# A convolution network's third stage: one-pass spreads of split statistics, and a group mean taken from integers instead of from the activations

## The chip, the cores and the metric

The kernel runs on one core of one Trainium2 chip. The metric is the device time of one launch in microseconds, the median of three runs. The core's engines are named as in the profile: PE (TensorE) multiplies matrices, PEld is its weight load, DVE is VectorE, ACT is ScalarE, POOL is GpSimd, and SP only issues DMAs here. Each engine works off its own instructions in order and waits on semaphores for the others.

## The reference

x has the shape (8192, 8, 16, 16): samples, channels, height, width. Four residual layers follow one another; each normalizes in four groups of two channels (512 values) and convolves.

```python
x = x + L0(_gn(x))   # tensor-train product, bias
x = x + L1(_gn(x))   # 3x3 convolution, batch norm, relu
x = x + L2(_gn(x))   # q = clip(round(gn * 127/max|gn|)), integer 3x3 weights, / (sx * sw), bias
x = x + L3(_gn(x))   # 3x3 convolution, edge padding, weights sign(w) * mean|w|, bias
# _gn: (g - mean) / sqrt(var + 1e-5) over each group of a sample
```

Layer 2 needs the largest magnitude of the whole normalized tensor, and layer 1's batch norm needs all of its output, so the work falls into three stages with a global step between them.

## The kernel before, in words

A batch tile is 128 samples: 128 partitions (8 channels x 16 rows) by 2048 columns (128 samples x 16 columns of the image). There are NT = 64 tiles. A 3x3 convolution is three matrix products with a 128x128 band matrix, one for each horizontal shift, so that a tile takes four quarters of 512 columns (`BANK`) times three products.

*Stage one* runs layer 0 and the convolution of layer 1 on every tile. Constants that are needed later are made a few at a time between its steps by `late_constants`. *Stage two* applies batch norm and relu, adds, takes each group's statistics, centres x by the group mean (so that a group of x has mean zero from there on), keeps the statistics in `gnst`, and finds the largest normalized magnitude. Thirteen tiles stay in SBUF, the others go through DRAM. *Stage three* runs layers 2 and 3 on every tile and writes the output.

What stage three does to a tile, by the names in its table `OPS`:

- `rows2`, `spread2`, `v`, `q`: the group's scale 1/sigma is turned from a column into rows on DVE (`to_rows`: products with a mask into `diag`, then a 32x32-block transpose), spread by PE over the 128 partitions into PSUM (`r2`, tile `ps_a`), and DVE multiplies x by it into int8. ACT turns the int8 into bf16 `q`.
- `c2h0`, `c2h1`: six bf16 products each make one half of layer 2 in PSUM (`pq`). `bias` adds layer 2's bias to the first half of x on ACT and `stz` adds the product to it on DVE; the second half is scaled and biased out of PSUM by ACT (`z1`, into `z3`) and added on POOL (`add1`).
- `sq`, `sums`: ACT squares x, and PE sums x and its square over a group's partitions (`s`): for each of four quarters one fp32 product with 32 output columns, each quarter in a 32-column tile of its own of the array. `small` on DVE reduces over the image's columns and turns the result; `pow` on POOL makes 1/sigma.
- `rows3`, `spread3`: mean/sigma, 1/sigma and the stage-two mean go to rows in the same way (three `diag` products and a transpose) and are spread by two fp32 products into `r3` (`ps_r`) and `o3` (`ps_o`).
- `t`, `hi`, `edl`, `lo`: x times 1/sigma is split into two fp32r parts, the high part by ACT and the low part by POOL. `c` and `corr` add the constant part to x. `c3h0a` to `c3h1b` are 24 fp32r products with the sign matrix (`pf`), and `out0`, `out1` on DVE add them to x; SP writes the tile out.

The order of all this is written out by hand. `PHASE` gives each operation a time within a tile, `PERIOD` the distance of tiles, and the operations of all tiles are issued in order of `PERIOD * i + PHASE[op]`. Each engine keeps that order, since its calls go through the helper `InOrder` (line 43, the line that the profile shows for nearly everything). In PSUM, `pq` and `pf` share two buffers of two banks (`pc`), and `hi`, `lo`, `v`, `q` and `t` have two buffers each. Loads of tiles from DRAM are issued by SP four tiles ahead, at the operation that begins a tile.

Of the kernel before, what the change touches and what calls it, by code (L numbers as in the profile page):

```python
# [18 lines left out]
P = 128  # L19
# [13 lines left out]
class InOrder:  # L33
# [24 lines left out]
PACK2 = [("w2all", C * C * 9), ("w3all", C * C * 9)]  # L58


@with_exitstack
def tile_net(ctx: ExitStack, tc: tile.TileContext, xb, xt_in, pack0, pack1, pack2, out):
# [34 lines left out]

    LATE = 5 if NT >= KEEP + STAY + 3 else 0

    def load2(i, what="yx"):  # L100
# [46 lines left out]
    def late_constants(late):  # L147
# [103 lines left out]
        dve.memset(gpad, 0.0)  # L251
        dve.tensor_copy(gpad[:, :, 0:G], quarter.unsqueeze(1).to_broadcast([P, NQ, G]))
        for k, name in enumerate(("sel0", "sel1", "corr")):

            t = L[name] = const.tile([P, CH], F32, name=name)
            dve.tensor_copy(t.rearrange("p (g n) -> p g n", g=G),
                            mod32[:, G * k:G * k + G].unsqueeze(2).to_broadcast([P, G, CH // G]))
        yield "statistics"
# [442 lines left out]

    def stats_small(mv, st, ps, name):

        s = small.tile([P, 32], F32, name=f"s_{name}", tag="s")
        dve.tensor_reduce(s, samples(ps), AX.X, ALU.add)
        dve.transpose(st, s)
        sq = small.tile([P, G], F32, name=f"sq_{name}", tag="sqm")
        dve.tensor_copy(mv[:, 0:G], st[:, 0:G])
        dve.tensor_tensor(sq, st[:, 0:G], mv[:, 0:G], ALU.mult)
        dve.scalar_tensor_tensor(mv[:, G:2 * G], st[:, G:2 * G], EPS, sq, ALU.add, ALU.subtract)  # L710

    def stats_pow(mv):
# [19 lines left out]
    with tc.tile_pool(name="p2", bufs=2) as p2, tc.tile_pool(name="ps2", bufs=2, space=PSUM) as ps2:  # L732
# [31 lines left out]
        def stats2(i):  # L764

            st, mv = psc[:, 32 + 32 * (i % 2):64 + 32 * (i % 2)], gnst[:, order2[i]]
            red = small.tile([P, 32], F32, name=f"s_c{i}", tag="s")
            dve.tensor_reduce(red, samples(T[i].pop("ps")), AX.X, ALU.add)
            dve.transpose(st, red)
            T[i]["sq"] = small.tile([P, G], F32, name=f"sq_c{i}", tag="sqm")  # L770
            act.copy(mv[:, 0:G], st[:, 0:G])
            act.activation(T[i]["sq"], st[:, 0:G], AF.Square)

        def sigma2(i):
            st, mv = psc[:, 32 + 32 * (i % 2):64 + 32 * (i % 2)], gnst[:, order2[i]]
            dve.scalar_tensor_tensor(mv[:, G:2 * G], st[:, G:2 * G], EPS, T[i].pop("sq"), ALU.add, ALU.subtract)
            stats_pow(mv)

        def spread2(i):
            T[i]["gb"] = ps = ps2.tile([P, BANK], F32, name=f"gb_{i}", tag="gb")  # L780
            rows = to_rows(diag[i % 2], mask2, [gnst[:, order2[i]]], f"c{i}")
# [46 lines left out]
        for i in range(NT + 4):  # L828
# [4 lines left out]
            elif late:  # L833
                k, j = late.pop(0)
                T2[j][k] = y_used[i - 1]
                nc.sync.dma_start(T2[j][k], (x1_d if k == "x" else y_d)[order2[j]])
            on(i, sum2)
            on(i - 2, sums2)
# [11 lines left out]
    nc.vector.tensor_reduce(pm, amax, AX.X, ALU.max)  # L850
    nc.gpsimd.partition_all_reduce(gm, pm, P, bass_isa.ReduceOp.max)
    nc.vector.reciprocal(sx, gm)
    nc.vector.tensor_scalar(sx, sx, 127.0, None, ALU.mult)
    nc.vector.tensor_tensor(inv, sx, L["sw"], ALU.mult)
    nc.vector.reciprocal(inv, inv)

    gv = gnst[:, :, G:2 * G]
# [5 lines left out]
    with ExitStack() as s:  # L863
        wk = s.enter_context(tc.tile_pool(name="wk3", bufs=2))
        ps_c = s.enter_context(tc.tile_pool(name="ps_c3", bufs=2, space=PSUM))
        ps_s = s.enter_context(tc.tile_pool(name="ps_s3", bufs=1, space=PSUM))
        order = [*kept, *(t for t in range(NT) if t not in kept)]

        sq3, t3, z3 = sqs[0], [sqs[1], xh], [y_stay[3][:, h * F // 2:(h + 1) * F // 2] for h in range(2)]
        T = [dict() for _ in range(NT)]  # L870
        AHEAD = min(NT, KEEP - 6)
        diag2, diag3 = diagonal("d"), diagonal("e")
# [3 lines left out]
        put_quarter(ps_a[:, P:2 * P])  # L876
        mask, st3 = ps_a[:, P:P + NQ], ps_a[:, P + 32:P + 64]

# [55 lines left out]
        def first2(i):  # L934
            x = halves(T[i]["x"])[:, 0]
            dve.scalar_tensor_tensor(x, T[i].pop(("pq", 0)), inv, x, ALU.mult, ALU.add)

        def second2(i):
            act.activation(z3[i % 2], T[i].pop(("pq", 1)), AF.Identity, bias=L["bias2"], scale=inv)

        def add2(i):
            x = halves(T[i]["x"])[:, 1]
            pool.tensor_tensor(x, x, z3[i % 2], ALU.add)

# [3 lines left out]
        def sums3(i):  # L948
            T[i]["ps"] = ps_s.tile([P, BANK], F32, name=f"s3_{i}", tag="s3")
            sums_pe(T[i]["ps"], T[i]["x"], sq3)  # L950

        def stats3(i):
            T[i]["mv"] = small.tile([P, 2 * G], F32, name=f"mv3_{i}", tag="mv")
            stats_small(T[i]["mv"], st3, T[i].pop("ps"), f"d{i}")

        def pow3(i):
            stats_pow(T[i]["mv"])

# [43 lines left out]
        def finish(i, h):  # L1002
# [8 lines left out]
        OPS = {"rows2": rows2, "spread2": spread2, "v": scale2, "q": round2, "bias": bias2,  # L1011
               "c2h0": lambda i: layer2(i, 0), "stz": first2, "c2h1": lambda i: layer2(i, 1), "z1": second2, "add1": add2,
               "sq": square3, "sums": sums3, "small": stats3, "pow": pow3, "rows3": rows3, "spread3": spread3, "c": offset3,
               "t": scale3, "hi": high3, "lo": low3, "corr": add3, "edl": edges3,
               "c3h0a": lambda i: layer3(i, 0, 0), "c3h0b": lambda i: layer3(i, 0, 1), "out0": lambda i: finish(i, 0),
               "c3h1a": lambda i: layer3(i, 1, 0), "c3h1b": lambda i: layer3(i, 1, 1), "out1": lambda i: finish(i, 1)}
        todo = [(op, i) for _, op, i in sorted((PERIOD * i + at, op, i) for op, at in PHASE.items() for i in range(NT))]
# [75 lines left out]
```

## Time and profile before

| what | value |
|---|---|
| median of three runs | 3823.76 us (3823.36 to 3825.31) |
| the profiled execution: time, span | 3824.58 us, 3822.8 us |
| mean granted clock of PE | 0.962 |
| busy in the span: PE, DVE, ACT, POOL | 94%, 89%, 66%, 80% |
| stage two's last operation on DVE (`amax`) | starts at 3062.76 us |
| third stage's first `v` | starts at 3066.51 us |

The span runs from the first to the last instruction. The share of busy time over the whole span is an average of three stages with different limits, so the table is only a start: a change in one stage is read from that stage's own stretch of time, its own chain of waits and its own timeline.

### The profile page before, as it was taken

The numbers are of one execution on the slowest core, as the hardware profiler recorded it, in microseconds if no ns is written. First come the engines' busy times: TensorE is split into PE (matmuls) and PEld (weight loads), VectorE is DVE, ScalarE is ACT, GpSimd is POOL, SyncE is SP. The second block draws the span as 40 slices with busy tenths as digits, with TensorE's granted clock in tenths as the row PEclk, the third lists the DMA queues.
The fourth block names the chain that finished last, engine by engine and source line by source line (L and its number), as shares of the span: only waits on it lengthen the run. The fifth ranks groups of instructions, "written<-read, shape, count | busy, mean of one in ns | idle before, by whom it ended". The sixth has DMA issues, their size and how long they took to land.

```text
span 3822.8 us, 52777 instructions
## 1 busy us (share of the span) xinstructions
PE 3598.8 (94%) x16264; PEld 2127.1 (56%) x16326; DVE 3386.0 (89%) x6313; ACT 2518.2 (66%) x2676; POOL 3048.8 (80%) x3104
## 2 busy tenths in 40 slices
PE   8999999999999999999999999997665589999999
PEld 4666666666666666666666666663221145555555
DVE  8988888888888888888888888877998889999997
ACT  5666666666666666666666666665665578778775
POOL 4877777778777777787777777865887779999998
PEclk9999999999999999999999999998776689999999
DMA  5787787878877878878788878766999724444442
GB/s 212 254 270 256 258 269 252 265 258 258 271 253 261 272 253 262 262 250 272 254 263 270 257 258 265 253 200 253 419 424 424 326 90 186 182 183 187 181 161 110
DMA packets 210809, 960.93 MB, mean 251 GB/s; under 512 B 44896, under 2 KB 45152, under 8 KB 110048
## 3 DMA queue, kind: packets, MB, share of 16 engines
q1 hardware_dynamic: 173808, 692.22, 48.8%
q0 software_dynamic: 36288, 264.26, 23.5%
q8 instruction: 131, 2.15, 0.2%
q14 instruction: 150, 1.23, 0.1%
q10 hardware_dynamic: 432, 1.08, 0.1%
HBM read 578.84 MB, written 378.54 MB: 250 GB/s over the span
## 4 chain that ended last, share of the span: by engine, by line
PE 85%; DVE 6%; DMA 4%; issue 2%; POOL 1%; ACT 1%; POOLq 0%; SPq 0%; DVEq 0%; ACTq 0%
PE po L43 45%; PE pu L43 12%; PE pf L43 10%; PE pm L43 6%; PE pq L43 4%; PE s L43 3%; PE pc L43 3%; DVE top L43 3%; PE ps_r L43 1%; DMA ys<-x_d 1%; DMA x_d<-u 1%; DMA x_d<-ys 1%; DMA u<-x_d 1%; DMA x_d<-xs 1%; DMA sq<-y_d 1%
## 5 line engine op out<-in xcount | busy, mean ns | idle before, releaser
L43 PE MATMUL po<-u,core 128*128 128x512 f32 (+1 forms) x4112 | 1844.7, 591 | 0.0
L43 ACT COPY u<-pu 128x2048 f32<-128x2048 f32 x512 | 955.4, 1866 | 512.9 <-PE pu L43 512.8
L43 PEld LDWEIGHTS po<-u,core 128*128 128x128 f32 x4112 | 744.6, 190 | 737.0 <-issue 736.1
L43 PE MATMUL pu<-core2r,xl 128*128 128x256 f32 x4032 | 678.6, 310 | 4.5 <-ACT u L43 3.5
L43 PEld LDWEIGHTS pu<-core2r,xl 128*128 128x128 f32 x4032 | 527.9, 189 | 127.9 <-issue 123.1
L43 POOL TENSOR_TENSOR bs<-bs,xh 128x512 fp32r<-128x512 f32 (+1 forms) x253 | 325.1, 1285 | 203.0 <-ACT xh L43 203.0
L43 POOL TENSOR_TENSOR v<-e 128x128 f32<-128x128 f32 x750 | 396.7, 540 | 0.0
L43 DVE TENSOR_TENSOR xs<-po,xs 128x512 f32<-128x512 f32 x256 | 176.9, 691 | 218.8 <-PE po L43 218.6
L43 ACT ACTIVATE m<-pm,b 128x128 f32<-128x128 f32 x250 | 91.7, 367 | 395.3 <-PE pm L43 395.3
L43 PEld LDWEIGHTS pm<-v,fast 128*128 128x128 f32 x2000 | 262.5, 192 | 119.7 <-issue 105.7
L43 POOL TENSOR_TENSOR e<-x1n,x 128x512 f32<-128x512 f32 x250 | 305.9, 1223 | 23.2 <-ACT x L43 15.8
L43 DVE TENSOR_TENSOR bs<-bs,stat 128x1024 f32<-128x1024 f32 x252 | 290.6, 1215 | 2.1
L43 POOL TENSOR_TENSOR xs<-xs,w 128x2048 f32<-128x2048 f32 x64 | 291.4, 4552 | 0.6 <-DMA xs<-in_xt 0.6
L43 PE MATMUL pm<-v,fast 128*128 128x128 f32 x2000 | 263.6, 275 | 0.0
L43 ACT ACTIVATE x<-x1n 128x512 f32<-128x512 f32 x500 | 247.0, 545 | 7.6 <-DVE x1n L43 7.6
L43 POOL TENSOR_TENSOR mv<-mv,mhalf 128x4 f32<-128x4 f32 x127 | 130.8, 1030 | 135.9 <-DVE mv L43 135.9
L43 PE MATMUL pf<-hi,sign 128*128 128x512 f32 x768 | 231.1, 439 | 0.0
L43 POOL DMA_DIRECT2D xl<-limb_d x252 | 149.8, 594 | 101.3 <-ACT x L43 38.4
L43 PE MATMUL pf<-lo,sign 128*128 128x512 f32 x768 | 218.0, 422 | 0.3 <-ACT lo L43 0.3
L43 POOL TENSOR_TENSOR v<-r 128x128 f32<-128x128 f32 x500 | 215.2, 447 | 0.0
L43 ACT ACTIVATE sq<-xs 128x2048 f32<-128x2048 f32 x103 | 197.0, 1913 | 18.2 <-DVE xs L43 13.6
L43 PE MATMUL gb<-rows_c,sel 128*128 128x128 f32 x128 | 40.8, 413 | 166.3 <-DVE rows_c L43 166.3
(308 smaller groups left out, 7195.3 us busy)
## 6 DMA issues: line engine op xcount, KB each, us to landing
xl<-limb_d POOLq DMA_DIRECT2D x252, 1024.0 KB, 7.4
x_d<-xs SPq DMA_DIRECT2D x76, 1024.0 KB, 8.4
xs<-in_xt SPq DMA_DIRECT2D x64, 1024.0 KB, 7.6
bs<-in_xb SPq DMA_DIRECT2D x63, 1024.0 KB, 5.6
limb_d<-xh SPq DMA_DIRECT2D x1008, 64.0 KB, 4.4
limb_d<-bs SPq DMA_DIRECT2D x1008, 64.0 KB, 5.2
y_d<-ys SPq DMA_DIRECT2D x60, 1024.0 KB, 8.0
u<-x_d SPq DMA_DIRECT2D x34, 1024.0 KB, 6.5
```

What stands on the lines that cost most here:

```text
L43: return self.tc.keep_in_program_order(op(*args, **kwargs))
```

## The change

**Statistics to rows.** Mean/sigma, 1/sigma, the stage-two mean of tile i and the scale of tile i + 4 (`LEAD`) are gathered as 16 columns (`columns3`, ACT; `shift3`, DVE). They are split into a high half that fp32r holds exactly (`high_column3`, ACT) and the rest (`low_column3`, DVE), 32 columns in all. One fp32r product with the identity turns them into 32 rows in PSUM (`turn3`), ACT copies these out (`rows3`), and four fp32r products with 32 rows spread them (`spread3`). The mask, the `diag` products and the transposes of both old spreads go.

**The mean of layer 3's input.** Since a group of x has mean zero before layer 2, the sum over a group comes from layer 2's integers: products of bf16 `q` with band matrices whose output columns are summed by group (`total`, made by `group_weights` in stage two), less what the image's two edge columns have too much. That is eight bf16 products of 512 columns and sixteen of 32 columns in place of the four fp32 products with x. The squares are summed as before. The group mean of the bias moves from layer 2's bias to layer 3's.

**Work moved between engines.** `SHARE` = 24 samples (384 columns) of layer 2's second half go the way of the first half: ACT's `bias` covers 1408 columns, DVE adds them (`third2`, named `stz1`), and `z1` and `add1` shrink to 640. The squared mean moves from DVE to ACT (`sqm`).

**Order.** `PHASE` and `PERIOD` are new, the second half of layer 2 and of layer 3 now comes ahead of the first, and the seven shared operations also run for tiles -4 to -1.

```diff
-PERIOD = 11.539
-PHASE = {"rows2": 0, "spread2": 0.01, "v": 5.1, "q": 10.2, "bias": 10.4, "c2h1": 11.6, "z1": 13.1, "c2h0": 16.1, "add1": 17.1,
-         "stz": 23.1, "sq": 24, "sums": 31.8, "small": 34.7, "pow": 37.3, "rows3": 42.7, "spread3": 45.3, "t": 46.3,
-         "hi": 49.9, "c": 51.2, "lo": 51.9, "corr": 58.8, "edl": 60.3, "c3h0a": 60.4, "c3h0b": 61.3, "out0": 66.8,
-         "c3h1a": 69.3, "c3h1b": 69.4, "out1": 69.41}
+PERIOD = 10.91
+PHASE = {"v": 0, "q": 5.5, "c2h1": 7.9, "bias": 10.7, "cols": 12.1, "stz1": 12.3, "c2h0": 13, "z1": 13.2, "stz": 14.4,
+         "add1": 16.1, "sq": 19, "sums": 20.4, "small": 24.9, "sqm": 26.2, "var": 26.21, "pow": 27.1, "mr": 29.5, "lhh": 31.8,
+         "lhl": 32.7, "turn": 33.6, "rows": 33.9, "spread": 36, "t": 37.2, "c": 43.8, "hi": 48.4, "lo": 49.3, "corr": 49.4,
+         "edl": 57.1, "c3h1a": 58.1, "c3h1b": 58.6, "c3h0a": 61, "c3h0b": 61.2, "out1": 62, "out0": 65.5}
+LEAD = 4
+SHARE = 24
...
+        pair = w["bias2all"].rearrange("p (g k) -> p g k", k=C // G)
+        dve.tensor_tensor(pair, pair, grp.unsqueeze(2).to_broadcast([P, G, C // G]), ALU.mult)
+        mb = const.tile([P, 1], F32, name="mb")
+        dve.tensor_reduce(mb, w["bias2all"], AX.X, ALU.add)
+        dve.tensor_scalar(mb, mb, 512.0 * G / C, None, ALU.mult)
+        dve.tensor_tensor(L["bias2"], L["bias2"], mb, ALU.subtract)
+        dve.tensor_tensor(L["bias3"], L["bias3"], mb, ALU.add)
...
+        def group_weights():
+            part = const.tile([P, 3, G], F32, name="part")
+            total = L["total"] = const.tile([P, 6, 32], BF16, name="total")
+            pool.memset(total, 0.0)
+            dve.tensor_reduce(part.rearrange("p k g -> p (k g)"), L["band2"].rearrange("p k (g n) -> p (k g) n", g=G), AX.X, ALU.add)
+            for k in range(0, 3, 2):
+                dve.tensor_tensor(part[:, 1], part[:, 1], part[:, k], ALU.add)
+                dve.tensor_scalar(part[:, k], part[:, k], -1.0, None, ALU.mult)
+            dve.tensor_copy(total[:, 0:3, 0:G], part)
+            dve.tensor_tensor(total[:, 3:6, 0:G], part, total[:, 0:3, 0:G], ALU.subtract)
...
     nc.gpsimd.partition_all_reduce(gm, pm, P, bass_isa.ReduceOp.max)
...
+    K3 = 8 * G
+    identr = wk.tile([P, P], F32R, name="identr", bufs=1)
+    back2, back3, high, low = (wk.tile([K3, CH], F32R, name=n, bufs=1) for n in ("back2", "back3", "corr_h", "corr_l"))
+    L["select"](back2, 3, 7)
+    L["select"](back3, 1, 5)
+    act.copy(high, L["corr"][0:K3])
+    act.copy(identr, ident)
+    dve.tensor_tensor(low, L["corr"][0:K3], high.bitcast(F32), ALU.subtract)
...
-        def rows2(i):
-            T[i]["rows2"] = to_rows(diag2[i % 2], mask, [gnst[:, order[i], G:2 * G]], f"d{i}")
+        def columns3(i):
+            T3[i] = col = wk.tile([P, 4 * G], F32, name=f"col_{i}", tag="col", bufs=4)
+            if i < 0:
+                for k in range(2):
+                    act.copy(col[:, 2 * G * k:2 * G * k + 2 * G], gnst[:, i + LEAD])
+            elif i + LEAD < NT:
+                act.copy(col[:, 2 * G:3 * G], gnst[:, i, 0:G])
+                act.copy(col[:, 3 * G:], gnst[:, i + LEAD, G:2 * G])
...
+        def shift3(i):
+            if i >= 0:
+                dve.scalar_tensor_tensor(column(i, 0), st3[:, 0:G], inv512, column(i, 1), ALU.mult, ALU.mult)
+
+        def high_column3(i):
+            act.copy(lhs[i % 2][:, 0:4 * G], T3[i])
+
+        def low_column3(i):
+            lh = lhs[i % 2]
+            dve.tensor_tensor(lh[:, 4 * G:], T3.pop(i), lh[:, 0:4 * G].bitcast(F32), ALU.subtract)
+
+        def turn3(i):
+            pe.matmul(turned, lhs[i % 2], identr, start=True, stop=True)
 
         def rows3(i):
-            mv = T[i].pop("mv")
-            mr = small.tile([P, G], F32, name=f"mr_{i}", tag="mr")
-            dve.tensor_tensor(mr, st3[:, 0:G], mv[:, G:2 * G], ALU.mult)
-            T[i]["rows3"] = to_rows(diag3[i % 2], mask, [mr, mv[:, G:2 * G], gnst[:, order[i], 0:G]], f"e{i}")
-
-
-        def spread2(i):
-            pe.matmul(r2, L["sel0"], T[i].pop("rows2"), start=True, stop=True)
+            T3["rows", i] = rows = wk.tile([K3, P], F32R, name=f"rows_{i}", tag="rows")
+            act.copy(rows, turned)
 
         def spread3(i):
-            rows = T[i].pop("rows3")
-            pe.matmul(r3, L["sel1"], rows, start=True, stop=True)
-            pe.matmul(o3, L["corr"], rows, start=True, stop=True)
+            rows = T3.pop(("rows", i))
+            if i + LEAD < NT:
+                pe.matmul(r2, back2, rows, start=True, stop=True)
+            if i >= 0:
+                pe.matmul(r3, back3, rows, start=True, stop=True)
+                for k, part in enumerate((high, low)):
+                    pe.matmul(o3, part, rows, start=(k == 0), stop=(k == 1))
...
         def bias2(i):
-            x = halves(T[i]["x"])[:, 0]
+            x = T[i]["x"][:, 0:F // 2 + SHARE * W]
             act.activation(x, x, AF.Identity, bias=L["bias2"], scale=1.0)
...
+        def third2(i):
+            x = halves(T[i]["x"])[:, 1][:, 0:SHARE * W]
+            dve.scalar_tensor_tensor(x, T[i]["pq", 1][:, 0:SHARE * W], inv, x, ALU.mult, ALU.add)
...
         def sums3(i):
             T[i]["ps"] = ps_s.tile([P, BANK], F32, name=f"s3_{i}", tag="s3")
-            sums_pe(T[i]["ps"], T[i]["x"], sq3)
+            ps, qs = T[i]["ps"], samples(T[i]["q"])
+            for j in range(2):
+                for k, w in ((1, slice(0, W)), (0, slice(W - 1, W)), (2, slice(0, 1))):
+                    for q in range(NQ):
+                        pe.matmul(samples(ps)[32 * q:32 * q + 32, :, w], L["total"][:, 3 * j + k],
+                                  qs[:, q * QS:(q + 1) * QS, w], start=(j == 0 and k == 1), stop=False)
+            for q in range(NQ):
+                pe.matmul(ps[32 * q:32 * q + 32], L["wsum"][:, 1], sq3[:, q * BANK:(q + 1) * BANK], start=False, stop=True)
...
+        def square_mean3(i):
+            T[i]["sqm"] = small.tile([P, G], F32, name=f"sqm_{i}", tag="sqm")
+            act.activation(T[i]["sqm"], st3[:, 0:G], AF.Square, scale=inv512)
+
+        def variance3(i):
+            dve.scalar_tensor_tensor(column(i, 1), st3[:, G:2 * G], EPS, T[i].pop("sqm"), ALU.add, ALU.subtract)
...
-            if op == "rows2" and AHEAD <= i + 4 < NT:
+            if op == "v" and AHEAD <= i + 4 < NT:
                 load3(i + 4)
```

More of the change, by code (lines that the diff above doesn't have):

```diff
@@ L44, in __getattr__ @@
         return call
-PERIOD = 11.539
-PHASE = {"rows2": 0, "spread2": 0.01, "v": 5.1, "q": 10.2, "bias": 10.4, "c2h1": 11.6, "z1": 13.1, "c2h0": 16.1, "add1": 17.1,
-         "stz": 23.1, "sq": 24, "sums": 31.8, "small": 34.7, "pow": 37.3, "rows3": 42.7, "spread3": 45.3, "t": 46.3,
-         "hi": 49.9, "c": 51.2, "lo": 51.9, "corr": 58.8, "edl": 60.3, "c3h0a": 60.4, "c3h0b": 61.3, "out0": 66.8,
-         "c3h1a": 69.3, "c3h1b": 69.4, "out1": 69.41}
+PERIOD = 10.91
[5 more added lines that the diff above has]
+SHARE = 24
 PACK0 = [("c0", R * C), ("c1", R * H), ("core2", 2 * R * W), ("bias0", W)]
 PACK1 = [("w1", 9 * C), ("core2r", 2 * R * W), ("linb", C), ("gamma", 1), ("beta", 1), ("w2", 9 * C), ("bias2", 1), ("w3", 9 * C), ("bias3", 1)]
-PACK2 = [("w2all", C * C * 9), ("w3all", C * C * 9)]
+PACK2 = [("w2all", C * C * 9), ("w3all", C * C * 9), ("bias2all", C)]
 @with_exitstack
@@ L98, in tile_net @@
     LATE = 5 if NT >= KEEP + STAY + 3 else 0
+    stays = order2[max(0, NT - KEEP - LATE):NT - LATE]
+    order = [*stays, *(t for t in range(NT) if t not in stays)]
+    place = {t: i for i, t in enumerate(order)}
     def load2(i, what="yx"):
@@ L251, in late_constants, with select @@
         dve.memset(gpad, 0.0)
[L252 to L257, printed above, removed]
+        for k in (0, 4 * G):
+            dve.tensor_copy(gpad[:, :, k:k + G], quarter.unsqueeze(1).to_broadcast([P, NQ, G]))
+        def select(t, *ks):
+            tv = t.rearrange("p (g n) -> p g n", g=G)
+            a = [mod32[0:t.shape[0], G * k:G * k + G].unsqueeze(2).to_broadcast([t.shape[0], G, CH // G]) for k in ks]
+            if len(a) == 1:
+                dve.tensor_copy(tv, a[0])
+            else:
+                dve.tensor_tensor(tv, a[0], a[1], ALU.add)
+        L["select"] = select
+        for name, ks in (("sel0", [0]), ("sel1", [1]), ("corr", [2, 6])):
+            L[name] = const.tile([P, CH], F32, name=name)
+            select(L[name], *ks)
         yield "statistics"
@@ L700, in put_quarter @@
         nc.vector.tensor_copy(ps[:, 0:NQ], L["quarter"])
[L702 to L710, printed above, removed]
     def stats_pow(mv):
@@ L764, in stats2 @@
         def stats2(i):
-            st, mv = psc[:, 32 + 32 * (i % 2):64 + 32 * (i % 2)], gnst[:, order2[i]]
+            st, mv = psc[:, 32 + 32 * (i % 2):64 + 32 * (i % 2)], gnst[:, place[order2[i]]]
             red = small.tile([P, 32], F32, name=f"s_c{i}", tag="s")
@@ L774, in sigma2 @@
         def sigma2(i):
-            st, mv = psc[:, 32 + 32 * (i % 2):64 + 32 * (i % 2)], gnst[:, order2[i]]
+            st, mv = psc[:, 32 + 32 * (i % 2):64 + 32 * (i % 2)], gnst[:, place[order2[i]]]
             dve.scalar_tensor_tensor(mv[:, G:2 * G], st[:, G:2 * G], EPS, T[i].pop("sq"), ALU.add, ALU.subtract)
@@ L780, in spread2 @@
             T[i]["gb"] = ps = ps2.tile([P, BANK], F32, name=f"gb_{i}", tag="gb")
-            rows = to_rows(diag[i % 2], mask2, [gnst[:, order2[i]]], f"c{i}")
+            rows = to_rows(diag[i % 2], mask2, [gnst[:, place[order2[i]]]], f"c{i}")
             if i % 4 == 0:
@@ L836, in tile_net @@
                 nc.sync.dma_start(T2[j][k], (x1_d if k == "x" else y_d)[order2[j]])
+            if i == 8:
+                group_weights()
             on(i, sum2)
@@ L851, in tile_net @@
     nc.gpsimd.partition_all_reduce(gm, pm, P, bass_isa.ReduceOp.max)
+    wk = ctx.enter_context(tc.tile_pool(name="wk3", bufs=2))
+    K3 = 8 * G
[6 more added lines that the diff above has]
+    dve.tensor_tensor(low, L["corr"][0:K3], high.bitcast(F32), ALU.subtract)
     nc.vector.reciprocal(sx, gm)
@@ L855, in tile_net @@
     nc.vector.reciprocal(inv, inv)
+    inv512 = const.tile([P, 1], F32, name="inv512")
+    nc.vector.tensor_scalar(inv512, inv, 1.0 / 512, None, ALU.mult)
     gv = gnst[:, :, G:2 * G]
@@ L863, in tile_net @@
     with ExitStack() as s:
-        wk = s.enter_context(tc.tile_pool(name="wk3", bufs=2))
         ps_c = s.enter_context(tc.tile_pool(name="ps_c3", bufs=2, space=PSUM))
         ps_s = s.enter_context(tc.tile_pool(name="ps_s3", bufs=1, space=PSUM))
-        order = [*kept, *(t for t in range(NT) if t not in kept)]
         sq3, t3, z3 = sqs[0], [sqs[1], xh], [y_stay[3][:, h * F // 2:(h + 1) * F // 2] for h in range(2)]
-        T = [dict() for _ in range(NT)]
+        T, T3 = [dict() for _ in range(NT)], {}
         AHEAD = min(NT, KEEP - 6)
-        diag2, diag3 = diagonal("d"), diagonal("e")
+        lhs = [wk.tile([P, K3], F32R, name=f"lh{k}", bufs=1) for k in range(2)]
         ps_a, ps_r, ps_o = (ps_s.tile([P, BANK], F32, name=f"ps_{n}", tag=n) for n in ("a", "r", "o"))
         r2, r3, o3 = ps_a[:, 0:P], ps_r[:, 0:P], ps_o[:, 0:P]
-        put_quarter(ps_a[:, P:2 * P])
-        mask, st3 = ps_a[:, P:P + NQ], ps_a[:, P + 32:P + 64]
+        st3, turned = ps_a[:, P:P + 32], ps_o[0:K3, P:2 * P]
         def load3(i):
@@ L903, in spread3 @@
-        def spread3(i):
-            rows = T[i].pop("rows3")
-            pe.matmul(r3, L["sel1"], rows, start=True, stop=True)
-            pe.matmul(o3, L["corr"], rows, start=True, stop=True)
+        def columns3(i):
[6 more added lines that the diff above has]
+                act.copy(col[:, 3 * G:], gnst[:, i + LEAD, G:2 * G])
+            else:
+                act.copy(col[:, 2 * G:], gnst[:, i])
@@ new lines, in column @@
+        def column(i, k):
+            return T3[i][:, k * G:(k + 1) * G]
+        def shift3(i):
[8 more added lines that the diff above has]
+            pe.matmul(turned, lhs[i % 2], identr, start=True, stop=True)
@@ L936, in first2 @@
             dve.scalar_tensor_tensor(x, T[i].pop(("pq", 0)), inv, x, ALU.mult, ALU.add)
+        def third2(i):
+            x = halves(T[i]["x"])[:, 1][:, 0:SHARE * W]
+            dve.scalar_tensor_tensor(x, T[i]["pq", 1][:, 0:SHARE * W], inv, x, ALU.mult, ALU.add)
         def second2(i):
-            act.activation(z3[i % 2], T[i].pop(("pq", 1)), AF.Identity, bias=L["bias2"], scale=inv)
+            act.activation(z3[i % 2][:, SHARE * W:], T[i]["pq", 1][:, SHARE * W:], AF.Identity, bias=L["bias2"], scale=inv)
         def add2(i):
-            x = halves(T[i]["x"])[:, 1]
-            pool.tensor_tensor(x, x, z3[i % 2], ALU.add)
+            x = halves(T[i]["x"])[:, 1][:, SHARE * W:]
+            pool.tensor_tensor(x, x, z3[i % 2][:, SHARE * W:], ALU.add)
         def square3(i):
@@ L949, in sums3 @@
             T[i]["ps"] = ps_s.tile([P, BANK], F32, name=f"s3_{i}", tag="s3")
-            sums_pe(T[i]["ps"], T[i]["x"], sq3)
-        def stats3(i):
-            T[i]["mv"] = small.tile([P, 2 * G], F32, name=f"mv3_{i}", tag="mv")
-            stats_small(T[i]["mv"], st3, T[i].pop("ps"), f"d{i}")
+            ps, qs = T[i]["ps"], samples(T[i]["q"])
[6 more added lines that the diff above has]
+                pe.matmul(ps[32 * q:32 * q + 32], L["wsum"][:, 1], sq3[:, q * BANK:(q + 1) * BANK], start=False, stop=True)
+        def stats3(i):
+            red = small.tile([P, 32], F32, name=f"s_{i}", tag="s")
+            dve.tensor_reduce(red, samples(T[i].pop("ps")), AX.X, ALU.add)
+            dve.transpose(st3, red)
+        def square_mean3(i):
[3 more added lines that the diff above has]
+            dve.scalar_tensor_tensor(column(i, 1), st3[:, G:2 * G], EPS, T[i].pop("sqm"), ALU.add, ALU.subtract)
         def pow3(i):
-            stats_pow(T[i]["mv"])
+            pool.tensor_tensor(column(i, 1), column(i, 1), mhalf[:, :G], ALU.pow)
         def offset3(i):
@@ L1009, in finish @@
                 T[i].clear()
-        OPS = {"rows2": rows2, "spread2": spread2, "v": scale2, "q": round2, "bias": bias2,
-               "c2h0": lambda i: layer2(i, 0), "stz": first2, "c2h1": lambda i: layer2(i, 1), "z1": second2, "add1": add2,
-               "sq": square3, "sums": sums3, "small": stats3, "pow": pow3, "rows3": rows3, "spread3": spread3, "c": offset3,
+        OPS = {"v": scale2, "q": round2, "bias": bias2,
+               "c2h0": lambda i: layer2(i, 0), "stz": first2, "c2h1": lambda i: layer2(i, 1), "stz1": third2, "z1": second2,
+               "add1": add2, "sq": square3, "sums": sums3, "small": stats3, "sqm": square_mean3, "var": variance3, "pow": pow3,
+               "cols": columns3, "mr": shift3, "lhh": high_column3, "lhl": low_column3, "turn": turn3, "rows": rows3,
+               "spread": spread3, "c": offset3,
                "t": scale3, "hi": high3, "lo": low3, "corr": add3, "edl": edges3,
@@ L1016, in tile_net @@
                "c3h1a": lambda i: layer3(i, 1, 0), "c3h1b": lambda i: layer3(i, 1, 1), "out1": lambda i: finish(i, 1)}
-        todo = [(op, i) for _, op, i in sorted((PERIOD * i + at, op, i) for op, at in PHASE.items() for i in range(NT))]
+        SHARED = ("cols", "mr", "lhh", "lhl", "turn", "rows", "spread")
+        todo = [(op, i) for _, op, i in sorted((PERIOD * i + at, op, i) for op, at in PHASE.items()
+                                              for i in range(-LEAD if op in SHARED else 0, NT))]
         for i in range(AHEAD):
@@ L1067 @@
         "w2all": everywhere(w2),
+        "bias2all": everywhere(L2_conv_bias),
         "bias2": rows(np.asarray(L2_conv_bias).reshape(C, 1), H),
```

## The prediction

> **What bounds the kernel now.** I first cut the span into stretches, to see which engine is full where. The columns are the stretch, its length, the busy time of PE, PEld, DVE, ACT and POOL (with instruction counts), the granted clock, the DMA share and GB/s.
>
> ```profile
> 2800.00:2900.00 100.00, 62.64 (x319) 21.10 (x320) 97.20 (x152) 60.74 (x62) 84.51 (x31) 0.70 1.01 425
> 3300.00:3400.00 100.00, 99.58 (x502) 59.04 (x510) 91.73 (x165) 80.31 (x70) 98.51 (x36) 1.00 0.48 181
> ```
>
> Up to about 3045 us the kernel is in stages one and two, which the change touches only with a few constants. The second stage has its DMA engines full (1.01) and DVE at 97%. The third stage (3065 to 3823) is a different regime: PE 99.6% busy at the full clock, POOL 98.5%, DMA half idle. Busy PE is not yet a bound, so the chain of waits in two of its periods comes next (start, us, what):
>
> ```profile
> 3395.94 6.15 PE pf L43 x24
> 3402.09 0.66 PE pq L43 x3
> 3402.75 0.05 issue
> 3402.80 0.60 PE pq L43 x2
> 3403.40 1.85 PE s L43 x16
> 3405.25 0.42 PE ps_r L43 x2
> 3405.67 0.22 PE ps_o L43 x2
> 3405.89 0.22 PE ps_a L43 x2
> 3406.12 1.30 PE pq L43 x6
> 3407.41 6.15 PE pf L43 x24
> ```
>
> Nothing but PE stands in it. One batch tile costs 6.15 (layer 3) + 1.31 + 1.30 (layer 2) + 1.85 (`s`, the sums) + 0.86 (three spreads) = 11.47 us, and the same line recurs every 11.47 us from 3109.05 to 3784.36, so 675.3/11.47 = 59 periods are set by PE alone. The timeline of PE splits the part that changes:
>
> ```profile
> 3403.33 1.06 PE L43 MATMUL s<-ys,wsum 128*32 128x512 f32 x8
> 3404.21 1.04 PE L43 MATMUL s<-sq,wsum 128*32 128x512 f32 x8
> 3405.18 0.49 PE L43 MATMUL ps_r<-rows_e,sel 128*128 128x128 f32 x2
> ```
>
> The sum of x takes 3403.33 to 3404.21, 0.88 us; the sum of squares 0.97 to the start of the spreads. POOL's timeline shows that it is full too:
>
> ```profile
> 3404.82 3.70 POOL L43 TENSOR_TENSOR xk<-xk,c 128x2048 f32<-128x2048 f32 x1
> 3408.47 1.03 POOL L43 TENSOR_TENSOR mv<-mv,mhalf 128x4 f32<-128x4 f32 x1
> 3409.46 2.42 POOL L43 TENSOR_TENSOR bs<-bs,bs 128x1024 f32<-128x1024 f32 x1
> 3412.06 4.28 POOL L43 TENSOR_TENSOR lo<-sq,hi 128x2048 fp32r<-128x2048 f32 x1 [0.18 <-ACT hi L43]
> ```
>
> 3.70 + 1.03 + 2.42 + 4.28 = 11.43 of 11.47. A faster PE alone would gain 0.04 us a tile; the change must relieve both.
>
> **What the Trainium skill says.** *FP8 and Floating Point Precision*, "TensorE Precision Notes": a true fp32 product takes four passes. The trace agrees: an fp32 128x512 of `s` shows two records, and a group of four column tiles takes about 0.43 us a record, two passes of 512; bf16 `pq` products start 0.216 us apart, fp32r `pf` 0.256 us apart (1.53 for six). *TensorE: Matmul & The Clock Gate*, "Part 3: Packing small matmuls — row/col tiling": products in different 32-column tiles run at once, about 4 ns apart; here they start 6 to 7 ns apart. *TensorEngine Tiling (Array Packing)*, "Key Properties": changing the tiling mode drains the array; here the last `pq` takes 0.31 instead of 0.216 before `s`, and the last group of `s` 0.52 instead of 0.43 before `ps_r`, so about 0.1 a switch. *TensorE: Matmul & The Clock Gate*, "Wait — 56ns, not 53.3ns?": starts are never under about 25 ns apart however small the product. No product of 32 columns is in this trace.
>
> **The change part by part, per tile, on PE.**
> - *Sum of x becomes a bf16 product of q.* Removed: 0.88. Added: two groups of four 128x512 at 0.216 = 0.43, and four groups of four with 32 moving columns. If the column tiles overlap as they do in `s`, a group costs about 0.03 (the floor above plus 7 ns steps): 0.55 in all. If each group shows its weight load (106 to 110 ns for 32 columns in the trace), 0.43 + 0.44 = 0.87. I take 0.60, nearer to the low end because the loads of `s` are hidden.
> - *Sum of squares.* The same four fp32 products, 0.97.
> - *Three fp32 spreads become one turn and four one-pass products of 32 rows.* Removed: 0.86, of which about 0.1 is the first exposed load, still paid. The nearest rows: a 128-column fp32 record (two passes of 128) follows the last after 0.11, and `pu` (fp32r, 256 columns) also after 0.115, since a 128-column load lasts about that. So an fp32r record of 128 columns cannot be cheaper than 0.11: four make 0.44. They stand between bf16 products of the whole array, and 32 rows may be another tiling mode: up to two switches, 0.64 in all. I take 0.55. The turn has 32 weight columns and follows the sums in their own mode: 0.05 to 0.15, I take 0.10.
>
> Together 0.60 + 0.97 + 0.10 + 0.55 = 2.22 where 2.71 stood: 0.49 less, a period of **10.98 us**.
>
> **The other engines.** POOL: `add1` shrinks from 1024 to 640 columns, 2.42 x 640/1024 = 1.51, so 10.52. ACT (80% busy, 9.2 us): the bias grows by 384 columns and the second evacuation shrinks by 384, which cancels (about 0.29 each, from 1.15 for 1024 and 1.91 for 2048); added are two `cols` copies, the high half, the rows (0.36 like `c`) and the squared mean; small ACT operations in stage two start 0.06 apart, so 0.6 in all: 9.8. DVE (91.7%, 10.5 us): off go four `diag` products, two 0.31 transposes, the copy and the square, by their starts 1.4 us; on come `third2` (384 of 1024 columns of a 1.24 product, about 0.55) and the low half (0.15): 9.8. None reaches 10.98, and removed `diag` work means DVE no longer stands just ahead of the spreads.
>
> The next thing late is a **ring**: `pf` of half one uses the PSUM buffer that `pq` of half one has just left, so it waits for ACT's evacuation, which in ACT's order stands behind `rows`, which waits for the turn. Its length: 6.15 + 1.30 (pq) + 1.57 (sums) + 0.10 (turn), then 0.3 until ACT sees it, 0.33 rows, 0.15 `cols`, 0.9 evacuation, 0.15 back to PE: 10.95. That fits within the period by nothing, so I allow no gain beyond about 0.6 us.
>
> **Once per run.** Before the first product of stage three, today: scaled gnst at 3065.0, diag, transpose, PE, then `v` at 3066.5. After: `cols` and high half on ACT, low half on DVE, turn, rows on ACT, spread, then `v`: added are a turn with its hop (0.7), rows on ACT with its hop (0.5) and three small operations with hops (0.75), gone are diag and transpose with theirs (0.65): +1.3 us. At the last tile the same exchange, where three diag products go (0.8), is +0.7, `cols` being early there. The selectors sit on DVE and ACT inside the wait for POOL's maximum (DVE idles 0.55 there): 0; if not, 0.5. `group_weights` puts seven small DVE operations into stage two, 1.5 us on a 97% busy DVE beside full DMA: between 0 and 1.5, I take 1.0. Eight small constant operations in stage one, where DVE is 88% busy and PE sets the pace: 0 to 1.2, I take 0.5. The moved load of the next tiles still goes out some 40 us ahead of its use against 4.8 us to landing: nothing, and if that lead were gone 5 us a tile. Behind `var`, which now waits for ACT's square, stands `t`; DVE has 1.2 us of slack a tile for that. Sum: +3.5.
>
> **Sum.** 59 x -0.49 + 3.5 = -25.4. The profiled execution took 3824.58 (span 3822.8), giving 3799.2; the median is 0.8 lower, so **3798.4 us**. Break-even is where sums, turn and spreads reach 2.71 - 3.5/59 = 2.65.
>
> **Rivals.**
> - *The ring binds instead of PE.* Should each of its four crossings cost 0.1 more than I allow, the period is 11.35, 0.12 less: -7 + 3.5, about 3820. For it: ACT is in strict order and `rows` stands ahead of the evacuation. Against: two of the crossings can overlap with `c` and the bias, already issued.
> - *Small products cost more than they replace.* Weight loads show in every group (0.87), and the four 32-row spreads, all on the same rows of the array, take load and product in turn, 0.2 each plus two switches (1.0); turn 0.15. 0.87 + 0.97 + 0.15 + 1.0 = 2.99, +0.28 a tile: +16.5 + 3.5, about 3844. For it: in the trace, after a switch, the second `ps_r` starts 0.213 after the first, load and product in turn. It decides above 2.65.
> - *Everything overlaps.* 0.55 + 0.97 + 0.05 + 0.44 = 2.01, -0.70; POOL's 10.52 and the ring stop it near 10.80: -39.5 + 2, about 3786.
>
> **Chances.** Forecast 0.58 (3790 to 3812), everything overlaps 0.10, ring 0.14, small products 0.18. A difference of 0.2% (7.6 us) is about what a measurement can tell from none: all of the first two and 0.06 of the ring are faster, the rest of the ring within, small products nearly all slower. The range, 3784 to 3833, takes in the ring and leaves out most of the last rival.
>
> **What would show it.** Right: `pf x24` recurring every 10.9 to 11.1 us, chain still nearly all PE; `s` about 1.6 us from first to last; `add1` at 1.5; POOL idle about 0.45 a tile. Wrong: PE waits ahead of `pf` on ACT's evacuation (ring); 32-column products 0.1 us apart or spreads at 0.2 each (small products); a stage two that ends over 2 us later.

## The result: 1.0% slower, and the profile after

| | before | after |
|---|---|---|
| median | 3823.56 us (4 runs) | 3861.45 us (3859.29 to 3870.64, 4 runs) |
| ratio to before, 95% interval | | 1.0103, 1.0086 to 1.0121 |
| profiled execution: time, span | 3824.58, 3822.8 us | 3863.49, 3861.7 us |
| first, last output transfer issued | 3113.54, 3817.68 us | 3127.60, 3856.61 us |
| distance of outputs, tiles 10 to 55 | 11.473 us | 11.885 us |

The forecast was 3798.4 with a range of 3784 to 3833: wrong in sign, and outside its range. The issue times of the 64 output transfers say where the 38.9 us of span went: 14.1 before the first output, 24.9 over the 63 distances after it, nothing after the last. Stages one and two show no cost: stage two's `amax` starts at 3061.54 (before 3062.76), and in the traces of experiments 1 to 5 and 10, which have the same first two stages, between 3061.35 and 3063.47, so a difference of 1 us is not told from none there.

The stretch of the third stage, with the columns of the prediction's first fence (length, then PE, PEld, DVE, ACT, POOL, clock, DMA share, GB/s):

```profile
3300.00:3400.00 100.00, 97.39 (x624) 56.67 (x630) 83.69 (x110) 81.25 (x109) 88.78 (x34) 1.00 0.46 177
```

No engine is full now: POOL fell from 98.5 to 88.8%, DVE from 91.7 to 83.7%, as the change intends, and yet the time rose. That is the mark of a ring, a closed sequence of waits through several engines. The chain of waits over one period (start, us, what) shows it:

```profile
3399.53 1.28 DVE u L43
3400.81 0.54 DVE xk L43
...
3401.37 0.88 ACT bs L43
3402.25 0.41 ACT lo L43
...
3402.93 1.82 ACT hi L43
...
3405.22 1.89 ACT q L43
3407.12 1.81 ACT sq L43
3408.93 0.10 ACT lh L43
...
3409.06 0.18 DVE lh L43
3409.23 1.44 DVE v L43 x2
3410.67 0.74 issue
3411.41 1.28 DVE u L43
```

There is no PE in it. DVE's addition of layer 3's output half (`out0`, 1.28) holds `stz1` (0.54) back; ACT's evacuation `z1` (`bs`) follows `stz1`; behind it ACT's list runs through edges, `hi`, `q` and `sq` to the high half (`lhh`, shown as `lh`); DVE's low half (`lhl`) waits for that, and DVE's `v` and the next `out0` stand behind the low half. 3411.41 - 3399.53 = 11.88, the period. (The 0.74 of "issue" is no wait: in DVE's timeline the two records of `v` run from 3409.15 to 3411.49, and `out0` starts at their end.) The DVE timeline gives the wait its number (idle before, and releaser, in brackets):

```profile
3409.06 0.18 DVE L43 TENSOR_TENSOR lh<-col,lh 128x16 fp32r<-128x16 f32 x1 [1.30 <-ACT lh L43]
```

In each tile DVE stands idle about 1.3 us ahead of an operation of 16 columns, with 2.3 us of `v` behind it; POOL's `add1` then waits 1.40 us for ACT's `z1`. PE's part, answering to the prediction's PE lines:

```profile
3410.54 0.86 PE L43 MATMUL s<-q,total 128*32 128x512 bf16 x24
3411.21 1.05 PE L43 MATMUL s<-sq,wsum 128*32 128x512 f32 x8
3412.19 0.25 PE L43 MATMUL ps_o<-identr,lh 128*32 128x128 f32 x1
3412.74 1.46 PE L43 MATMUL pq<-q,band 128*128 128x512 bf16 x5 [0.31 <-DVE u L43]
3414.22 0.29 PE L43 MATMUL ps_a<-rows,back 32*128 32x128 f32 x1
```

From start to start the sum of x takes 0.67, the squares 0.98. PE's only wait in the period is the 0.31 us ahead of `pq`, for `out0` to free the PSUM buffer. The fill (up to the first output) shows one more thing, in DVE's and POOL's timelines:

```profile
3106.01 3.72 DVE L43 TENSOR_TENSOR lh<-col,lh 128x16 fp32r<-128x16 f32 x1 [3.25 <-ACT lh L43]
```

```profile
3106.02 3.68 POOL L43 TENSOR_TENSOR u<-u,c 128x2048 f32<-128x2048 f32 x1
```

The same 16 columns that take 0.18 elsewhere lasted 3.72 us, from the start of POOL's `corr` to its end; the one at 3120.55 lasted 3.44 beside a `corr` of 3.69. The Trainium skill, *SBUF — State Buffer*, "SBUF: two separate sides", says how this can be: GpSimd and VectorE share a pair of ports, held exclusively for a whole instruction, and a VectorE operation with two SBUF inputs needs that pair against a GpSimd operation that reads SBUF. The low half reads `col` and the high half, both in SBUF. The old `diag` products had their mask in PSUM, so they did not meet it.

### The profile page after: what moved, and what is told of

The parts are those of the page before. It is cut to its first block, busy times and chain, and to the rows that moved or that the text cites. A ratio compares the mean times of both kernels' runs of the same rounds, so it can differ in the third digit from the quotient of the medians.

```text
span 3861.7 us, 54830 instructions
## 1 busy us (share of the span) xinstructions
PE 3601.4 (93%) x17227; PEld 2126.3 (55%) x17290; DVE 3365.1 (87%) x5949; ACT 2558.3 (66%) x3010; POOL 2997.5 (78%) x3101
## 4 chain that ended last, share of the span: by engine, by line
PE 67%; DVE 12%; ACT 12%; DMA 5%; issue 3%; POOL 1%; POOLq 0%; SPq 0%; DVEq 0%; ACTq 0%
PE po L43 44%; PE pu L43 12%; PE pm L43 6%; ACT q L43 3%; ACT hi L43 3%; PE pc L43 3%; ACT sq L43 3%; DVE v L43 2%; DVE top L43 2%; ACT bs L43 1%; DVE xs L43 1%; DVE u L43 1%; DMA u<-x_d 1%; DVE ys L43 1%; PE pf L43 1%
## 5 line engine op out<-in xcount | busy, mean ns | idle before, releaser
L43 ACT ACTIVATE m<-pm,b 128x128 f32<-128x128 f32 x250 | 91.7, 367 | 395.2 <-PE pm L43 395.2
L43 PE MATMUL pq<-q,band 128*128 128x480 bf16 (+1 forms) x705 | 188.2, 387 | 31.8 <-ACT q L43 10.8
```

The source lines that it names most:

```text
L43: return self.tc.keep_in_program_order(op(*args, **kwargs))
```

## The experiments

The theory after these readings: (A) **order**: the ring above sets the period, since `lhh` stands behind `sq` on ACT and `lhl` ahead of `v` on DVE. Rivals: (B) **port**: the low half is blocked by POOL wherever it stands. (C) **PE**: the small products cost more than they replace. All ratios are to the kernel before, with 95% intervals.

**1. The order alone.** The high half goes ahead of `sq` on ACT (it stays behind `q`), the shift ahead of `out1` on DVE, and the low half right behind `out1`:

```diff
-"mr": 29.5, "lhh": 31.8, "lhl": 32.7
+"mr": 29.2, "lhh": 29.9, "lhl": 29.95
```

> Changed kernel with three times of its plan moved: the split's high half goes ahead of the square on ACT, the shift ahead of out1 on DVE, the low half right behind out1, so that v no longer waits for ACT's square. Theory 'order': the changed kernel's 11.88 us period is a ring of ACT (z1, edges, sqm, hi, q, sq, high half) and DVE (low half, v, out0, stz1) through the low half's place. Then the period falls to what PE needs without its one stall of 0.25 us a tile, 11.64, and the time by 59 x 0.24 = 14, to about 3847. Rival 'shared port': the low half is DVE's only product in this stage with both inputs in SBUF and cannot run while POOL's lo runs; placed earlier it stands blocked until lo ends, its record grows from 0.18 to about 1.5 us, v starts as late as now, and the time stays within 4 us of 3861.

Measured: 3856.04, ratio 1.0082 (1.0067 to 1.0097), period 11.850. The period is as the rival said; the time is 5.4 us less than after, mostly in the fill (first output at 3121.62 instead of 3127.60). B holds here: the ring A opened, and another closed at nearly the same length. The group of low halves (minimum/median/maximum ns) and the chain:

```profile
L43 DVE TENSOR_TENSOR lh<-col,lh x64: 176/1697/1981, 3085.0 to 3823.9; 128x16 fp32r<-128x16 f32 x64
```

```profile
3399.49 1.28 DVE u L43
3400.78 1.59 DVE lh L43
3402.37 1.56 DVE v L43 x2
```

The low half that ends at 3402.37 ends with POOL's `lo` (3398.06, 4.28 us long). So the new ring is the old one with POOL's `lo` in place of ACT's edges, `q`, `sq` and high half, and in the changed kernel the two ways are equally long: `hi` ends at 3404.75, ACT's high half at 3409.03, and `lo` takes 4.28 as well. DVE is 96.4% busy in this stretch, 12.7 points more than after: a blocked operation counts as busy.

**2. Order and port.** ACT writes a second copy of the high half into a free part of a PSUM tile, and the low half reads that, so one of its inputs is in PSUM:

```diff
+            act.copy(ps_o[:, 2 * P + 16 * (i % 2):2 * P + 16 * (i % 2) + 16].bitcast(F32R), T3[i])
...
-            dve.tensor_tensor(lh[:, 4 * G:], T3.pop(i), lh[:, 0:4 * G].bitcast(F32), ALU.subtract)
+            dve.tensor_tensor(lh[:, 4 * G:], T3.pop(i), ps_o[:, 2 * P + 16 * (i % 2):2 * P + 16 * (i % 2) + 16], ALU.subtract)
```

> The same three moves, and the low half reads the high half from PSUM, where ACT writes a second copy of it (0.1 us of ACT a tile). Theory 'shared port' with 'order': with one input in SBUF nothing blocks the low half; the period falls to PE's 11.64, and the two stalls of 3.7 and 3.4 us of the stage's start go: 3861 - 14 - 7 = 3840. Theory 'order' alone: the same as the run without the PSUM copy. Not below 11.6 a tile, if PE's turn and spreads cost what the trace of after shows.

Measured: 3831.65, ratio 1.0019 (1.0012 to 1.0026), period 11.426. The low half takes 160 ns (157 to 172 over 64 tiles), the chain is all PE again, PE 100% busy. So A and B were both true. The period is below my 11.64, which took off only PE's visible idle time: from the turn to the next `pq` it is 0.09 from start to start here, 0.55 in the PE lines of after. Yet PE alone is now only 0.05 below the old 11.473: C also holds, in part. From its chain:

```profile
3407.38 0.25 PE ps_a L43
...
3407.97 6.39 PE pf L43 x24
```

Its terms are s 1.65, turn 0.18, spreads 0.58 = 2.41 where I had 2.22, and `pf` at 6.39.

**3. The spreads over the whole array.** `rows` and the selectors get 128 partitions, 96 of them zero, so that the spreads are 128x128 products like their neighbours and, if 32 rows are a tiling mode of their own, the mode does not change. First alone on the changed kernel:

```diff
-    back2, back3, high, low = (wk.tile([K3, CH], F32R, ...
+    back2, back3, high, low = (wk.tile([P, CH], F32R, ...
...
+    for z in (back2, back3, high, low, *rows2):
+        act.copy(z, zero)
...
-            act.copy(rows, turned)
+            act.copy(rows[0:K3], turned)
```

> Changed kernel, spreads over 128 rows (rows 32 and up are zeros on both sides), so that the four products do not change the array's tiling mode. Nothing else is changed. If the ring through ACT and DVE sets the period, PE's saving (0.15 before the spreads and up to 0.1 behind them) becomes PE idle time: 11.88 a tile, time within 4 us of 3861. If PE sets it, 59 x 0.15 to 0.25 = 9 to 15 us faster.

Measured: 3863.02, ratio 1.0098 (1.0081 to 1.0115), period 11.892: nothing, as a ring without PE demands.

**4. All three together.**

> The three moves, the low half's PSUM input and the spreads over 128 rows together. If order and port set the period first and PE's mode switches stand behind them: 11.64 - 0.15 to 0.25 = 11.4 to 11.5 a tile, about 3826 to 3832 us. If the mode switches cost nothing: as the run without full rows.

Measured: 3813.61, ratio 0.9972 (0.9962 to 0.9982), period 11.106: faster than before, and below the 11.4 to 11.5 that I expected from 11.64. One period of its chain:

```profile
3402.39 6.27 PE pf L43 x24
3408.65 1.31 PE pq L43 x6
3409.96 1.65 PE s L43 x29
3411.61 0.18 PE ps_o L43
3411.78 1.31 PE pq L43 x6
3413.10 0.06 PE ps_a L43
3413.16 0.11 PE ps_r L43
3413.27 0.22 PE ps_o L43 x2
```

Sums, turn and spreads are 1.65 + 0.18 + 0.39 = 2.22, and `pf` fell from 6.39 to 6.27: the 32-row form cost 0.19 + 0.12 = 0.31 a tile, and 11.426 - 11.106 = 0.32 is what its removal gave. The ends of PE's records are modelled, so the starts are the better guide to where it lay: from the last `pq` to the second spread 0.47 us falls to 0.28, from the last spread to the second `pf` 0.56 to 0.42, and the spreads between stand 0.11 apart in both. The 96 rows of zeros cost nothing; the two passages between 32 rows and the whole array did. That they are a drain at a change of mode, as the prediction supposed, fits this but is not seen as such in a trace.

**5. The port alone** (the PSUM copy, with the order of the changed kernel).

> Changed kernel in its own order, only the low half reads the high half from PSUM. In the steady part the low half is not blocked there (0.18 us), it only waits for ACT, so the order's ring of 11.88 us a tile should stay. The two stalls of 3.7 and 3.4 us at the stage's start and the two of 1.2 and 1.4 us at its end should go: 7 to 10 us faster than the changed kernel, 3852 to 3855. If port alone were the cause, the period would fall to 11.43 and the time to about 3832.

Measured: 3862.29, ratio 1.0099 (1.0084 to 1.0115), period 11.953: not the 7 to 10 us faster that I expected. The low half takes 171 ns everywhere and the first output comes 4.4 us earlier (3123.18), but the period is longer by 0.07, about ACT's extra copy (0.08), which lies in the ring, and the two cancel. With experiment 1 this shows that order and port each hold the period near 11.9 alone; removing one does nothing.

**6. The setup moved into stage two.** Experiment 4's kernel, with its selectors and zeros made in stage two:

> The run with all of the three moves, the PSUM input and the spreads over 128 rows; the selectors and their zeros are made in stage two instead of between the stages. There DVE's first low half stood at 3066.5 us instead of 3064.6, so about 1.5 us less: 3812, period unchanged at 11.11. If stage two has no room for them, no gain.

Measured: 3812.61, ratio 0.9970 (0.9959 to 0.9981), first output at 3121.62 instead of 3121.96: nothing that stands out of the intervals.

**7. The mean from q in the old order.** Does the bf16 sum work without the new spreads? The kernel before gets `total`, the bf16 products and the adapted biases; here with the smaller `add1` (`SHARE` 24) too:

> Kernel before with its own order, spreads and DMA, plus two parts of the change: the mean from bf16 products of q, and 24 samples of the second half moved from POOL and z1 to DVE. PE theory: the sums take 1.65 instead of 1.85 us, POOL has 0.9 us of room, so 11.47 falls to 11.27 a tile: 59 x 0.20 = 12 less, 1 to 2 more for the constants, about 3814. Rival: the DVE addition of 0.6 us, standing where it does in the old order, holds up the first half's addition or the scaling and eats it: 3820 or more.

Measured: 3945.27, ratio 1.0318 (1.0303 to 1.0333), period 13.40: the expectation failed. **8.** The mean alone, without `SHARE`:

> Kernel before plus the mean from bf16 products of q alone; POOL keeps its 11.43 us a tile. POOL should now be the bound: 11.43 to 11.47 a tile, 0 to 3 us less and 1 to 2 us more for constants: 3822 to 3826. If POOL can be overlapped further than its records say, as the run with the share.

Measured: 3839.47, ratio 1.0040 (1.0025 to 1.0055), period 11.755: failed too. The group of ACT's `q` says what was missed (busy, mean ns, then idle before it and releaser):

```profile
L43 ACT CAST q<-v 128x2048 bf16<-128x2048 int8 x9 | 17.1, 1899 | 25.3 <-PE s L43 25.3
```

25.3/9 = 2.8 us a tile: `q` has two buffers, and the sums now read it too. In the old order `q` of the next tile but one is due at 10.2 + 2 x 11.54 = 33.3, when the sums placed at 31.8 are barely through; in the changed kernel's order it is due at 5.5 + 2 x 10.91 = 27.3, long after the sums at 20.4. (In experiment 7 it was 35.7/8 = 4.5; the share with a third buffer was not run.) That this is what the time hangs on was tested next:

**9. The mean alone, with three buffers for q.**

```diff
-            q = wk.tile([P, F], BF16, name=f"q_{i}", tag="q")
+            q = wk.tile([P, F], BF16, name=f"q_{i}", tag="q", bufs=3)
```

> The kernel before with the bf16 sum of x, as in the run that did this alone (3839.47, period 11.755), and one thing more: three buffers for q instead of two. Theory (in that run ACT's rounding of q waited about 2.8 us a tile for PE's sums, because they now hold the q buffer of two tiles ago): the wait goes, PE needs about 11.25 us a tile, and POOL's 11.43 binds: period 11.43 to 11.48, 3821 to 3826, the chain with POOL or PE in it and ACT's q without a wait of PE's s. Rival (the wait for q only showed where PE stood anyway, and the order of PE's sums and layer 2 costs the time): period stays 11.7 to 11.8, about 3839.

Measured: 3814.08, ratio 0.9974 (0.9964 to 0.9984), period 11.333. The wait is gone, and the gain is larger than the 3821 to 3826 that I expected: the chain is all PE (6.21 + 1.31 + 1.65 + 0.86 + 1.30 = 11.33), with POOL's unchanged operations inside 11.33. Its timeline shows how:

```profile
3400.47 3.74 POOL L43 TENSOR_TENSOR xk<-xk,c 128x2048 f32<-128x2048 f32 x1
3404.13 1.06 POOL L43 TENSOR_TENSOR mv<-mv,mhalf 128x4 f32<-128x4 f32 x1
3405.12 2.46 POOL L43 TENSOR_TENSOR bs<-bs,bs 128x1024 f32<-128x1024 f32 x1
3407.49 4.32 POOL L43 TENSOR_TENSOR lo<-sq,hi 128x2048 fp32r<-128x2048 f32 x1
3411.72 3.73 POOL L43 TENSOR_TENSOR xk<-xk,c 128x2048 f32<-128x2048 f32 x1
```

The durations add up to 3.74 + 1.06 + 2.46 + 4.32 = 11.58, but the next round starts 11.25 us after the first: a POOL record overlaps the next by 0.07 to 0.1. Without a gap POOL goes round in 11.2 to 11.25 until about 3560 us, where it has caught up with PE, and in 11.33 from there. My 11.43 for POOL was a sum of records, not its floor.

**10. Experiment 4's kernel without the bf16 mean.**

```diff
-            ps, qs = T[i]["ps"], samples(T[i]["q"])
...
+            sums_pe(T[i]["ps"], T[i]["x"], sq3)
```

> The kernel with the high half copied into PSUM, the new places of shift, high and low half, and spreads over 128 rows (3813.61, period 11.106), with one part of the change undone: the sum of x by fp32 products with x again, with scales to match. Theory (PE is the only bound there, and the bf16 sum is worth what the records show, 0.88 - 0.667 = 0.21 us a tile): period 11.31 to 11.33, 3813.6 + 63 x 0.21 = about 3827, the chain all PE with s 1.85. Rival (other engines' orders bind just under PE, so that most of the 0.21 is lost in waits anyway): period at most 11.2, 3814 to 3820. If instead x's release by the sums holds something up, more than 11.4 and over 3832.

Measured: 3824.85, ratio 1.0003 (0.9994 to 1.0011), period 11.295, s 1.85 in an all-PE chain: the mean is worth 0.19 a tile, 11.2 us, close to the 0.21 of the records.

So the two parts of the change have separate accounts. The bf16 mean with a third buffer for `q` is nearly the whole gain of the best versions (experiment 9: -0.26%; experiment 6: -0.30%). The spreads, mended and with the order and the shares that came with them, gain 11.473 - 11.295 = 0.18 a tile and give it back in a longer fill (first output 3121.90 against 3113.54), so that they end at no difference (experiment 10).

## Why the prediction was wrong, point by point

Two steps failed. "None reaches 10.98" summed the busy times of DVE and ACT and followed one ring through PE; a ring through DVE and ACT alone set the period, at 11.88. And turn and spreads, which the sum had 0.21 cheaper than before (0.65 for 0.86), came out 0.16 dearer with their passages to `pq` and `pf`, so that PE alone needs 11.43 and not 10.98 (experiment 2). Besides, the longer fill, 14.1 us, was put at nothing.

- **The bound of before.** PE alone in the chain: right. "The change must relieve both": wrong, since experiment 9 leaves POOL's work as it was and still runs at 11.33. The prediction's own POOL line has 0.18 of idle time before `lo`, which a slack of 0.04 cannot hold. That `add1` shrinks to 1.51 was right (1.57), but bought nothing.
- **Sum of x, squares.** 0.667 and 0.98 for 0.60 and 0.97: right in kind, a little low. The four groups with 32 moving columns took 0.03 to 0.06 each and showed no weight load, so the rival's 0.87 was far off. Within a group the four products start 2 to 4 ns apart, so the floor of 25 ns that the prediction builds on does not hold between column tiles.
- **Turn and spreads.** 0.18 + 0.58 for 0.10 + 0.55, and `pf` 6.39 for the 6.15 I left untouched. The term mis-sized is the switch of mode: I priced it from `s`, at about 0.1, and let it count only inside the spreads. It cost 0.32 a tile, some of it on the way back to `pf`. With 2.41 + 0.24 = 2.65 PE stood exactly at my break-even: this step alone took the gain away, as experiment 2 shows. With the switches gone, my sum of 2.22 was reached, but by luck, since its terms are others (1.65 + 0.18 + 0.39). The mended kernel's 11.106 is still 0.13 above 10.98, and that stands in `pf`, 6.27 for 6.15: from its second product to the next `pq` it takes 5.89 us before, and 5.94 to 5.97 after and in all experiments but 7, where it waits. Why is open.
- **"None reaches 10.98", and the ring.** This is the step that made it slower. I added up busy times for DVE and ACT (9.8 each; after, 83.7% and 81.3% of 11.88 are 9.9 and 9.7, so the sums were right) and followed one ring, PE's evacuation through `rows` and turn, because the old chain was PE's. The ring that bound has no PE in it. Two facts in the diff would have led to it: `lhh` at 31.8 stands behind `q` and `sq` of later tiles on ACT, and `lhl` at 32.7 ahead of `v` (3 x 10.91 = 32.73) on DVE. I priced the low half at 0.15 and never asked what it waits for or who is behind it, as I did for `var`.
- **The port.** The 0.15 was also a price without a neighbour. In the changed kernel the port set only the fill (4.4 us, experiment 5), since `lo` ends just as the low half may start; in the mended order it held the period.
- **Once per run.** First product of stage three: `amax` to `v` is 4.70 for 3.75, +0.95, where I said +1.3. Stages one and two: no sign of the 1.0 and 0.5, but the traces scatter by more. (Stage two runs to `amax` at 3062.76, not to 3045; no sum rests on it.) Tail: the last six distances of outputs add up to 51.6 for 50.1, +1.5 for 0.7. Missing altogether was the **fill**, 14.1 us. Experiments 1, 2, 4 and 5 take 4.4 to 8.4 of it away. The 8.4 that remain in experiment 4 stay open: its first four starts of `q` are 6.2, 7.4 and 8.3 apart where before they are 5.9, 5.7 and 5.7, so the new order seems to let fewer tiles in at first, but no run undid this alone.
- **Rivals.** "Small products cost more" had the right sign and named the switches, but its 3844 came from loads that did not show. No rival contained the mechanism that decided.

## What to carry to other kernels

When an order written by hand is changed, take every new small operation that waits for another engine, write down what stands ahead of the producer and what stands behind the consumer, and follow that path until it closes; the old chain of waits shows only the old rings, and busy shares show none. A few small products of another shape than their neighbours can cost more than the same padded with zeros to the neighbours' shape (here 0.32 us a tile for four). When an operation starts to read an old buffer, count that buffer's rounds again before judging the idea: here a third buffer turned +0.4% into -0.26%.

## What the runs showed of the hardware

- A DVE operation with two SBUF inputs, 16 columns wide, lasted up to 3.72 us beside a POOL operation, ending with it; with one input in PSUM 0.16 to 0.18 us. In the record the blocked time looks busy (DVE 96.4% for 83.7%).
- Four fp32r spreads of 32 rows between whole-array products cost 0.32 us a tile more than the same four over 128 rows: about 0.20 on the way into them and 0.14 on the way out, none between them.
- POOL's records overlap: start to start 11.25 us where the durations add up to 11.58.
